# Splitting weights and context by way of a PSUM bank, in a decoder layer with a fusion layer behind it

## The chip, the cores and the metric

The kernel runs on one core of a Trainium2 chip. Its engines are TensorE (PE in the profile, with its weight loads as PEld), VectorE (DVE), ScalarE (ACT), GpSimd (POOL) and SyncE (SP), which here only issues transfers. The metric is device time in microseconds (us) of one execution. Before the change the median of three runs was 2229.88 us (2228.8 to 2230.53).

## The reference

The input `x` is 4 x 1024 x 512 in fp32, the context 4 x 64 x 512. A decoder layer comes first: self-attention with 16 heads of 32, causal, on a normalised `x`; attention to the context; a feed-forward part of width 2048. A fusion layer follows.

```python
xn1 = _ln(x, g1, be1)
sa = _mha(xn1, xn1, Wq_s, bq_s, Wk_s, bk_s, Wv_s, bv_s, causal=True)
x = x + (sa @ W1 + b1)
xn2 = _ln(x, g2, be2)
ca = _mha(xn2, encoder_out, Wq_c, bq_c, Wk_c, bk_c, Wv_c, bv_c, causal=False)
x = x + (ca @ W2 + b2)
xn3 = _ln(x, g3, be3)
ff = jax.nn.relu(xn3 @ Wf1 + bf1) @ Wf2 + bf2
return x + ff
```

The fusion layer projects the result with `Wt`, gates it with `Wg` (whose second half meets a pooled and projected context) and normalises the sum. Scores are divided by `DH ** -0.5`, so they are multiplied by about 5.7 before the softmax.

## The kernel before

Most products are made in three matmuls. Each operand is split into a high part, rounded to the type `fp32r`, and a low part, the rest; high x high, high x low and low x high are summed in one PSUM bank. A split is two instructions: ACT casts the source to the high part, and DVE subtracts the high part from the source (`split`, lines 70 to 74). Where the source is the result of a matmul it lies in PSUM. Where it is a weight or the context it lies in SBUF, and both operands of the subtraction are read from there.

The kernel has three phases: self-attention (0 to about 930 us), attention to the context, and the feed-forward and fusion part (from about 1,330 us). The change touches the first alone.

Self-attention has 32 units: four sequences, four groups of four heads, two sets of four row tiles. For each unit `maxima` makes scores (line 673) and their extremes on DVE (lines 678 and 681), `attend` makes the transposed scores (729), exponentials on ACT (734), a causal cut and a sum over key blocks on POOL (742 and 783) and the product with the values (759). The maxima of one unit, the attention of the one before and pieces of the projections for later units (`pk`, `pq`, `pv`, line 101) are traced interleaved by `run`, by their share of matmul columns. A planner then orders the instructions of each engine by a simulated timeline and each step's place in the trace; on the chip every engine works through its own queue in that order.

PSUM has eight banks. In this phase four belong to the tag `s` (pool `ps_s`, line 450), three to the transposed scores and one to the product with the values. Tiles of one tag take the banks in the order in which they were traced, and a tile waits until the last reader of the tile four places before it is done. The helper `psum` (467) hands out banks for projections and set-up; from line 857 on they are all of the tag `s`, shared with the maxima.

Two groups of splits of SBUF data lie beside the attention:

- `split_steps` (248 to 259): W1, Wq_c (with a sign of -1) and W2, four chunks of 128 x 512 each. A step loads a chunk through SP's queue into a tile `low`, makes `high` on ACT (255) and `low` in place on DVE (256), and stores both to DRAM through SP (258). The twelve steps are appended to the projection pieces from `pieces[8]` on, one per piece (894 and 895), together with steps that clear other DRAM tiles (897).
- the late set-up, in the last four units: `Stream` (line 280 issues its transfers) brings chunks of Wt, Wg, the context, Wk_c and Wv_c through ACT's queue into a ring of five tiles. `halve` (313) and `load_context` (389) split 16 weight chunks and four context chunks of 128 x 256 with `split`; then the products of the set-up are made. A ring tile is free for the next transfer when its last reader is done, which for these chunks is the subtraction on DVE.

The pieces of one unit's fill are traced behind each other, so that a step's place in the trace also sets which tiles of the tag `s` stand before and behind it.

Of the kernel before, what the change touches and what calls it, by code (L numbers as in the profile page):

```python
# [11 lines left out]
AF = mybir.ActivationFunctionType  # L12
ALU = mybir.AluOpType
# [5 lines left out]
B, T, C, H = 4, 1024, 512, 16  # L19
DH = C // H  # L20
S = 64
# [24 lines left out]
def raw(ap):  # L46

    return ap.bitcast(F32)
# [3 lines left out]
def decoder_then_fusion(ctx: ExitStack, tc: tile.TileContext, x, ctxT, cols, rows,  # L52
                        Wq_s, Wk_s, Wv_s, W1, Wq_c, Wk_c, Wv_c, W2, Wf1, Wf2,
                        Wt, WvT, WgT, out):
    nc = tc.nc
# [5 lines left out]
    def chunks(w):  # L61
        return w.rearrange("(c p) n -> p c n", p=P)
# [8 lines left out]
    def split(hi, lo, src, uid, lo_eng=None):  # L71

        latest["hi"] = nc.scalar.copy(hi, src).ins  # L73
        (lo_eng or nc.vector).tensor_tensor(lo, src, hi, ALU.subtract)  # L74

    def split_biased(hi, lo, src, bias):

        nc.scalar.activation(hi, src, AF.Identity, bias=bias)
        nc.vector.scalar_tensor_tensor(lo, src, bias, hi, ALU.add, ALU.subtract)
# [10 lines left out]
    def product_steps(psum_of, a, b, a_at, b_at, width, end, bias=None):  # L90


        held = {}

        def step(c):
            if c == 0:
                held["ps"] = psum_of()
                if bias:
                    nc.tensor.matmul(held["ps"], *bias(), start=True, stop=False)
            for k, (i, j) in enumerate(((0, 0), (0, 1), (1, 0))):  # L100
                nc.tensor.matmul(held["ps"], a_at(a()[i], c), b_at(b()[j], c),  # L101
                                 start=not bias and c == 0 and k == 0, stop=c == NC - 1 and k == 2)
            if c == NC - 1:
                end(held["ps"])

        per = Z["per"]

        def steps(c):
            for i in range(c, c + per):
                step(i)  # L110

        return [(3 * width * per, lambda c=c: steps(c)) for c in range(0, NC, per)]
# [21 lines left out]
    def behind(*engines):  # L134

        stack = ExitStack()
        for eng in engines:
            last = next(i for i in reversed(nc.cur_bb.bb.instructions) if i.engine == eng.engine)
            stack.enter_context(tc.issue_after(last))
        return stack  # L140
# [16 lines left out]
    def col(name, c):  # L157
        at = COL_AT[name] + c
        return colv[:, at : at + 1]
# [48 lines left out]
    def spread_keys(k, part):  # L208

        src = part.rearrange("p c (b s) -> p c b s", s=S)  # L210
        for r in range(HG):
            at = slice(r * DH, (r + 1) * DH)
            nc.sync.dma_start(kbd_dram[k, :, at, :, r * S : (r + 1) * S].rearrange("b p c s -> p c b s"), src[at])

    def spread_values(i, t):

        src = t.rearrange("p (n r d) -> p n r d", r=2, d=DH)
        for m in range(2):
            for k in range(2):
                nc.sync.dma_start(vbd_dram[k * S : (k + 1) * S, i * 2 + m, :, k * DH : (k + 1) * DH],  # L220
                                  src[m * S : (m + 1) * S, :, k, :])
# [23 lines left out]
    SPLIT = {"w1": (W1, 1.0), "wqc": (Wq_c, -1.0), "w2": (W2, 1.0)}  # L245
    split_dram = {k: dram.tile([P, 2, NC, C], F32, tag=f"{k}_d", name=f"{k}_d") for k in SPLIT}

    def split_steps(pool, slots):

        def step(name, c):  # L250
            w, sign = SPLIT[name]
            low, high = [pool.tile([P, C], FR, tag="chunk", name=f"{name}_{k}_{c}", bufs=slots) for k in "lh"]
            with behind(nc.sync):
                nc.sync.dma_start(raw(low), chunks(w)[:, c, :])
            nc.scalar.activation(high, raw(low), AF.Copy, scale=sign)
            nc.vector.scalar_tensor_tensor(low, raw(low), sign, high, ALU.mult, ALU.subtract)
            for k, t in enumerate((high, low)):
                nc.sync.dma_start(split_dram[name][:, k, c], raw(t))
        return [(0, lambda name=name, c=c: step(name, c)) for name in SPLIT for c in range(NC)]
# [38 lines left out]
    def setup(psum, rows_pool, stream):  # L298
# [9 lines left out]
        def halve(pool, name, tag, c):  # L308

            if c == 0:  # L310
                held[name] = [pool.tile([P, NC, C], FR, tag=f"{tag}{k}", name=f"{name}{k}") for k in range(2)]
            hi, lo = held[name]
            stream.take(lambda src: split(hi[:, c], lo[:, c], src, f"{name}_{c}"))

        def halve_small(name, src):

# [6 lines left out]
        def put(ps, m, bias, dst, uid):  # L323

            out_row = rows_pool.tile([P, C], F32, tag="side", name=f"side_{uid}", bufs=2)
            if bias is None:
                nc.vector.tensor_copy(out_row[:m], ps[:m])
            else:
                nc.vector.tensor_tensor(out_row[:m], ps[:m], held[bias][:m], ALU.add)
            held[f"row_{uid}"] = out_row  # L330
            if callable(dst):
                dst(out_row)
            else:
                nc.sync.dma_start(dst, out_row[:m])
# [48 lines left out]
        def context(pool):  # L383
            def load_context(c):
                if c == 0:
                    held["kcT"] = [pool.tile([P, NC, B * S], FR, tag=f"kcT{k}", name=f"kcT{k}") for k in range(2)]
                    held["ct"] = [pool.tile([P, NC, B * S], FR, tag=f"ct{k}", name=f"ct{k}") for k in range(2)]
                hi, lo = held["ct"]
                stream.take(lambda src: split(hi[:, c], lo[:, c], src, f"ct_{c}"))

            def keys(ps, g):
                split_biased(held["kcT"][0][:, g], held["kcT"][1][:, g], ps, col("bk_c", g))
                if g == NC - 1:
                    for k, t in enumerate(held["kcT"]):
                        spread_keys(k, raw(t))

            steps = [(0, lambda c=c: load_context(c)) for c in range(NC)]
            steps += [(0, lambda c=c: halve(pool, "wkc", "w", c)) for c in range(NC)]
            for g in range(NC):
                steps += product_steps(  # L400
                    lambda g=g: psum(f"pkc_{g}")[:, : B * S], lambda: held["wkc"], lambda: held["ct"],
                    lambda w, c, g=g: w[:, c, g * P : (g + 1) * P], lambda t, c: t[:, c, :], B * S,
                    lambda ps, g=g: keys(ps, g))
            steps += [(0, lambda c=c: halve(pool, "wvc", "w", c)) for c in range(NC)]
            for i in range(B * S // P):
                steps += product_steps(
                    lambda i=i: psum(f"pvc_{i}"), lambda: held["ct"], lambda: held["wvc"],
                    lambda t, c, i=i: t[:, c, i * P : (i + 1) * P], lambda w, c: w[:, c, :], C,
                    lambda ps, i=i: put(ps, P, "bv_c", lambda t: spread_values(i, t), f"vc{i}"))
            return steps  # L410
# [27 lines left out]
    def self_attention(ph):  # L438
# [16 lines left out]
        ring = ph.enter_context(tc.tile_pool(name="ring_a", reuse_waits="tile", bufs=1))  # L455
        stream = Stream(ring, Z["ring"])
# [10 lines left out]
        def psum(name):  # L467

            kind = early_banks[len(psum_count) % len(early_banks)]
            psum_count.append(name)  # L470
            return ps_of[kind][0].tile([P, TG], F32, tag=kind, name=name)
# [419 lines left out]
                stream.fill()  # L891


        for i, step in enumerate(split_steps(ring, Z["ring"])):
            pieces[2 * NC + i].append(step)
        pieces[Z["pf"]].append((0, prefetch))
        for i, step in enumerate(clear_steps(mask[:, : HG * S])):
# [651 lines left out]
    for phase in (self_attention, cross_attention, feed_forward):  # L1549
        with ExitStack() as ph:  # L1550
            phase(ph)
# [41 lines left out]
```

## Time and profile before

| | before |
|---|---|
| median of three runs | 2229.88 us |
| the profiled execution | 2229.15 us |
| its span, first to last instruction | 2227.4 us |
| mean granted clock of PE | 0.981 |
| PE, DVE, ACT, POOL busy | 2121.6, 1255.2, 983.7, 1070.6 us |
| line 255, high parts of w1, wqc, w2, on ACT | 12 instructions, 7.5 us |
| line 256, their low parts, on DVE | 12 instructions, 14.8 us |
| line 73, high parts of wt, wgt, wkc, wvc, ct | 20 instructions, 11.4 us |
| line 74, their low parts, on DVE | 20 instructions, 26.7 us |

The rows of the last four lines are sums over the groups of these tiles. The page of the profile lists engines, 40 slices of the span, transfers, the chain of waits and the costliest groups. A row of a group or of a source line names the line, the engine, the operation, output `<-` inputs, the count and the durations; a row of the timeline starts with start and duration in us and ends in brackets with the idle time before it and what ended it. `st`, `s`, `pT`, `top` and `least` are tiles of the attention. A granted clock of 1.00 is full speed of PE.

### The profile page before, as it was taken

How to read it: one execution, taken by the hardware profiler on the slowest of the kernel's cores; microseconds unless marked ns; L12 is line 12 of the kernel's file. 1: busy time of each engine (PE TensorE's matmuls, PEld its weight loads, DVE VectorE, ACT ScalarE, POOL GpSimd, SP SyncE). 2: the span in 40 equal slices, each digit the busy share in tenths (PEclk: the TensorE clock that was granted, in tenths of full speed). 3: DMA queues.
4: the chain of work that ended last, by engine and by line, in shares of the span. 5: the costliest groups of instructions: out<-in, count | busy, mean ns of one | idle time of the engine just before them, and what ended most of it. 6: DMA issues, size and time to landing. Idle time of an engine off the chain costs nothing.

```text
span 2227.4 us, 34074 instructions
## 1 busy us (share of the span) xinstructions
PE 2121.6 (95%) x11736; PEld 1606.5 (72%) x11736; DVE 1255.2 (56%) x2800; ACT 983.7 (44%) x2175; POOL 1070.6 (48%) x1139
## 2 busy tenths in 40 slices
PE   6899999999999999989999998999999999999997
PEld 5667665666666755558888886888887887888785
DVE  6566756765665578666677756341337225431727
ACT  3355545554655455435555565432233324232432
POOL 3178777787878778765555523010115103410414
PEclk9999999999999999999999999999999999999998
DMA  8856766676656467662323214644345525442631
GB/s 251 241 157 172 238 194 206 192 221 191 192 151 189 136 168 221 201 205 67 101 80 104 80 50 154 197 166 141 124 139 207 170 98 202 145 175 85 207 134 48
DMA packets 219427, 356.24 MB, mean 160 GB/s; under 512 B 33516, under 2 KB 101852, under 8 KB 217206
## 3 DMA queue, kind: packets, MB, share of 16 engines
q1 hardware_dynamic: 201548, 333.83, 48.0%
q10 hardware_dynamic: 17706, 20.24, 2.9%
q8 instruction: 93, 1.52, 0.3%
q14 instruction: 80, 0.66, 0.1%
HBM read 242.27 MB, written 111.18 MB: 159 GB/s over the span
## 4 chain that ended last, share of the span: by engine, by line
PE 67%; DMA 10%; DVE 10%; issue 6%; POOL 4%; ACT 3%; SPq 1%; DVEq 0%; ACTq 0%; POOLq 0%
PE ph_f L101 13%; PE acc_f L1331 13%; PE s L673 4%; PE st L729 4%; PE av L759 4%; PE po_c L101 3%; PE pq_x L101 3%; PE pk L101 3%; PE pg_o L101 3%; PE pq L101 3%; PE po_x L101 3%; POOL pT L783 3%; PE pv L101 2%; PE sc_c L86 2%; PE den L796 1%
## 5 line engine op out<-in xcount | busy, mean ns | idle before, releaser
L783 POOL TENSOR_TENSOR pT<-pT,pT 128x256 f32<-128x256 f32 (+3 forms) x369 | 547.4, 1504 | 98.4 <-PE av L759 85.0
L1331 PE MATMUL acc_f<-wf,hs_f 128*128 128x512 f32 x1536 | 384.9, 394 | 7.6 <-DVE hs_f L74 5.9
L734 ACT ACTIVATE pT<-st 128x512 f32<-128x512 f32 (+2 forms) x640 | 317.2, 561 | 158.0 <-PE st L729 101.3
L101 PE MATMUL ph_f<-xn_f,wf 128*128 128x512 f32 x1536 | 381.7, 393 | 3.3 <-DVE xn_f L74 2.6
L1331 PEld LDWEIGHTS acc_f<-wf,hs_f 128*128 128x128 f32 x1536 | 285.0, 188 | 71.0 <-DVE hs_f L74 8.1
L101 PEld LDWEIGHTS ph_f<-xn_f,wf 128*128 128x128 f32 x1536 | 287.8, 189 | 65.0 <-DVE xn_f L74 3.0
L678 DVE CUSTOM_DVE_ANT_0 s<-s,mask 128x512 f32<-128x512 f32 (+3 forms) x512 | 245.8, 502 | 118.8 <-PE s L673 118.0
L673 PE MATMUL s<-ks,qs 96*128 96x512 f32 (+3 forms) x768 | 250.8, 375 | 28.4 <-DVE top L681 8.3
L1310 ACT ACTIVATE ph_f<-ph_f,colv 128x512 f32<-128x512 f32 x128 | 84.4, 659 | 391.3 <-PE ph_f L101 387.2
L74 DVE TENSOR_TENSOR hs_f<-ph_f,hs_f 128x512 fp32r<-128x512 f32 x128 | 87.9, 686 | 285.6 <-ACT hs_f L73 285.6
L729 PE MATMUL st<-qs,ks 98*128 98x256 f32 (+2 forms) x888 | 231.1, 342 | 12.2 <-DMA qs<-mT 6.6
L681 DVE TENSOR_REDUCE top<-s 128x1 f32<-128x512 f32 x256 | 175.6, 686 | 108.5 <-PE s L673 108.1
L673 PEld LDWEIGHTS s<-ks,qs 96*128 96x128 f32 x768 | 140.5, 194 | 107.3 <-DVE top L681 23.1
L729 PEld LDWEIGHTS st<-qs,ks 98*128 98x128 f32 x888 | 150.0, 193 | 65.3 <-ACT pT L734 24.7
L1306 POOL TENSOR_TENSOR y_f<-y_f,row_bf 128x512 f32<-128x512 f32 x32 | 42.0, 1317 | 313.8 <-DMA y_f<-x 253.9
L742 POOL TENSOR_SCALAR_AFFINE_SELECT pT<-pT 128x256 f32<-128x256 f32 x256 | 106.0, 431 | 126.1 <-ACT pT L734 92.6
L759 PE MATMUL av<-pT,v 128*32 128x512 f32 (+3 forms) x1776 | 157.2, 455 | 5.1 <-POOL pT L742 4.6
L1446 POOL TENSOR_TENSOR g_o<-g_o,z_o 128x512 f32<-128x512 f32 x28 | 41.8, 1506 | 175.7 <-DVE g_o L1445 172.9
L101 PE MATMUL pv<-wv,xn_s 128*128 128x256 f32 x768 | 107.5, 290 | 6.7 <-ACT vout L578 5.4
L101 PEld LDWEIGHTS pv<-wv,xn_s 128*128 128x128 f32 x768 | 100.4, 194 | 18.3 <-ACT vout L578 6.0
L1082 POOL TENSOR_TENSOR p_c<-p_c,inv_c 128x512 f32<-128x512 f32 x64 | 68.8, 1076 | 87.1 <-DVE inv_c L1081 65.2
L101 PE MATMUL pk<-xn_s,wk 128*128 128x512 f32 x384 | 104.0, 412 | 1.6 <-ACT xn_s L73 0.8
(220 smaller groups left out, 3397.0 us busy)
## 6 DMA issues: line engine op xcount, KB each, us to landing
wf<-wf2d SPq DMA_DIRECT2D x84, 512.0 KB
ks<-kd SPq DMA_DIRECT2D x96, 256.0 KB
qs<-qd SPq DMA_DIRECT2D x96, 256.0 KB
kd<-k SPq DMA_DIRECT2D x64, 256.0 KB
qd<-q SPq DMA_DIRECT2D x120, 128.0 KB
wf<-wf1d SPq DMA_DIRECT2D x28, 512.0 KB
x<-in_x SPq DMA_DIRECT2D x32, 256.0 KB
wk<-wk SPq DMA_DIRECT2D x16, 512.0 KB
```

The lines of the kernel that those rows point to most:

```text
L74: (lo_eng or nc.vector).tensor_tensor(lo, src, hi, ALU.subtract)
L101: nc.tensor.matmul(held["ps"], a_at(a()[i], c), b_at(b()[j], c), start=not bias and c == 0 and k == 0, stop=c == NC - 1 and k == 2)
L673: nc.tensor.matmul(sc[:, :w], q_at[u][:KS, r, j * P : (j + 1) * P], k_at[u, m][:KS, r, :w], start=True, stop=True)
L678: nc.vector.tensor_tensor_reduce(sc[:, :w], sc[:, :w], mask[:, TG - w :], 1.0, TOP, ALU.add, ALU.min, dst)
L681: nc.vector.tensor_reduce(dst, sc, AX.X, ALU.min)
L729: nc.tensor.matmul(st[:, i], k_at[u, kb // NJ][:KM, r + i, (kb % NJ) * P : (kb % NJ + 1) * P], q_at[u][:KM, r + i, c0:], start=True, stop= ...
L734: nc.scalar.activation(held[kb][(r + i) // 2][:, at : at + k, c0:], st[:, i : i + k], AF.Exp, scale=-QSCALE)
L742: nc.gpsimd.affine_select(out=t, in_=t, compare_op=ALU.is_ge, fill=0.0, base=0, pattern=[[0, 2], [1, P]], channel_multiplier=-1)
L759: return nc.tensor.matmul(held["av"][r * DH : (r + 1) * DH, c0:], v_at[b, g][:, kb, r * DH : (r + 1) * DH], held[kb][r // 2][:, r % 2, c0: ...
L783: eng.tensor_tensor(t[:, :, c0:], t[:, :, c0:], p[:, :, c0:], ALU.add)
L1310: nc.scalar.activation(ps, ps, AF.Relu, bias=col("bf1", f))
L1331: mm = nc.tensor.matmul(acc[j], held[f][i0][:, j * P : (j + 1) * P], w[2, f][:, i1], start=f == 0 and m == 0, stop=last and m == 2)
```

## The change

A new helper `split_over` copies the source to a PSUM tile with a scale on ACT, and then calls `split` with that tile as the source. ACT thus makes the copy and the high part, DVE subtracts the high part from the tile in PSUM. It takes the place of the two instructions in `split_steps` and of `split` in `halve` and `load_context`. Each call takes a tile of `psum`, hence of the tag `s`. The sign, where there is one, goes into the copy.

```diff
+    def split_over(ps, hi, lo, src, uid, sign=1.0):
+
+
+        nc.scalar.activation(ps, src, AF.Copy, scale=sign)
+        split(hi, lo, ps, uid)
...
-    def split_steps(pool, slots):
+    def split_steps(pool, slots, psum):
...
-            nc.scalar.activation(high, raw(low), AF.Copy, scale=sign)
-            nc.vector.scalar_tensor_tensor(low, raw(low), sign, high, ALU.mult, ALU.subtract)
+            split_over(psum(f"{name}_{c}"), high, low, raw(low), f"{name}_{c}", sign)
...
-            stream.take(lambda src: split(hi[:, c], lo[:, c], src, f"{name}_{c}"))
+            stream.take(lambda src: split_over(psum(f"{name}_{c}"), hi[:, c], lo[:, c], src, f"{name}_{c}"))
...
-                stream.take(lambda src: split(hi[:, c], lo[:, c], src, f"ct_{c}"))
+                stream.take(lambda src: split_over(psum(f"ct_{c}")[:, : B * S], hi[:, c], lo[:, c], src, f"ct_{c}"))
...
-        for i, step in enumerate(split_steps(ring, Z["ring"])):
+        for i, step in enumerate(split_steps(ring, Z["ring"], psum)):
```

## The prediction

> **What bounds the kernel now.** I read the busy times first, then the two lines that the change rewrites, then the idle gaps of TensorE (PE) around them in the timelines, and last the granted clock there. The page and the timeline of VectorE (DVE), for one stretch in the attention:
>
> ```profile
> PE 2121.6 (95%) x11736; PEld 1606.5 (72%) x11736; DVE 1255.2 (56%) x2800; ACT 983.7 (44%) x2175; POOL 1070.6 (48%) x1139
> ...
> 355.12 4.99 DVE L256 SCALAR_TENSOR_TENSOR wqc_l<-wqc_l,wqc_h 128x512 fp32r<-128x512 f32 x1 [2.26 <-ACT wqc_h L255]
> ```
>
> PE is busy in 95% of the span, so only its idle time and its slow clock can be won. That one subtraction took 4.99 us, and its twin at 338.7 us took 0.69. The timelines of POOL and PE for the same stretch say why, and what it did:
>
> ```profile
> 353.26 5.95 POOL L783 TENSOR_TENSOR pT<-pT,pT 128x1024 f32<-128x1024 f32 x3
> ...
> 360.77 1.22 PE L673 MATMUL s<-ks,qs 96*128 96x512 f32 x2 [3.07 <-DVE top L681]
> ```
>
> POOL ran three additions back to back until 359.2, and the subtraction ended 0.9 us later. The score matmul of PE waited 3.07 us for the maximum queued behind it. The whole family, from the views of the two lines (min/median/max ns):
>
> ```profile
> L256 DVE SCALAR_TENSOR_TENSOR w_l<-w_l,w_h x8: 674/692/1223, 224.0 to 530.5; 128x512 fp32r<-128x512 f32 x8
> L256 DVE SCALAR_TENSOR_TENSOR wqc_l<-wqc_l,wqc_h x4: 689/1550/4994, 338.7 to 425.1; 128x512 fp32r<-128x512 f32 x4
> ...
> L74 DVE TENSOR_TENSOR xn_s<-tpn_s,xn_s x32: 656/692/694, 13.7 to 656.9; 128x512 fp32r<-128x512 f32 x32
> ...
> L74 DVE TENSOR_TENSOR wt<-chunk,wt x4: 681/946/2407, 819.5 to 835.7; 128x512 fp32r<-128x512 f32 x4
> L74 DVE TENSOR_TENSOR wgt<-chunk,wgt x4: 685/1599/2964, 820.1 to 839.5; 128x512 fp32r<-128x512 f32 x4
> ...
> L74 DVE TENSOR_TENSOR ct<-chunk,ct x4: 630/1150/1497, 866.3 to 871.3; 128x256 fp32r<-128x256 f32 x4
> L74 DVE TENSOR_TENSOR wkc<-chunk,wkc x4: 674/769/1754, 871.9 to 880.2; 128x512 fp32r<-128x512 f32 x4
> L74 DVE TENSOR_TENSOR wvc<-chunk,wvc x4: 886/1633/2650, 894.5 to 899.6; 128x512 fp32r<-128x512 f32 x4
> ```
>
> The `xn_s` row reads one operand from PSUM and never exceeds 694 ns, though POOL works through the same stages. The others read both operands from SBUF and are held. Busy time and clock by stretch:
>
> ```profile
> core 0: us, PE busy (x) PEld busy (x) DVE busy (x) ACT busy (x) POOL busy (x), PEclk, DMA share, GB/s
> ...
> 180.00:540.00 360.00, 337.43 (x2208) 232.70 (x2208) 229.91 (x651) 185.76 (x373) 274.48 (x287) 0.97 0.71 205
> 540.00:815.00 275.00, 270.20 (x1807) 187.11 (x1806) 174.05 (x531) 148.80 (x299) 220.86 (x224) 1.00 0.59 166
> 815.00:905.00 90.00, 80.65 (x469) 52.30 (x468) 72.98 (x153) 48.11 (x97) 74.26 (x64) 0.92 0.74 214
> ```
>
> The 12 splits of w1, wqc and w2 lie in the first stretch, the 20 of the late set-up in the third, none in the second. PE idles 6% and 10% of the time where splits are, 2% where none are. In the third stretch DVE is 81% busy and ScalarE (ACT) 53%.
>
> **What is removed.** The 32 subtractions cost 41.5 us of DVE in the table of groups (w_l 6.0, wqc_l 8.8, wt 5.0, wgt 6.8, ct 4.3, wkc 3.9, wvc 6.7). From PSUM they should cost 28 x 0.69 + 4 x 0.43 = 21.0 us (0.69 is the `xn_s` median; 0.43 the mean of the 128x256 maxima that read PSUM, 434 ns). DVE gives back 20.5 us. Of that only what PE waits for counts. The timelines of PE and DVE show idle time of PE right behind a held subtraction; from each gap I take no more than the excess of that subtraction over 0.69 us: 3.07 (at 357.7), 1.37 of 1.62 and 0.2 of 0.76 (823.6 to 826.4), 1.22 and 0.45 of 0.68 (837.6 to 840.7), 0.77 and 1.26 of 1.85 (870.5 to 874.1), 0.83 (898.3). Sum 9.2 us.
>
> The clock comes on top. The granted clock was 0.50 from 358.3 to 368.5, 826.0 to 832.8 and 873.8 to 880.6 us, each time just behind such gaps, with 7.73 + 6.37 + 6.49 = 20.6 us of PE busy in them. At full clock that work takes half, so 10.3 us are at stake. I take 5.1, the middle, because other gaps (0.97 us for a transfer of mT at 355) lie beside the held ones.
>
> Two gains I count at nothing. POOL's additions are stretched too (128x512: 1,283 ns before 815 us, 1,382 after; 128x1024: 2,400 and 2,553): some 7 us of POOL over its 64 rows there, hidden because PE waits for POOL under 1 us in that stretch. And a ring slot of a context or weight chunk comes free at the new ACT copy, not at the end of the DVE subtraction, so ACT, whose queue issues the next chunk's transfer, no longer stops for DVE: waits of 2.9, 1.7, 0.9, 0.8 and 0.6 us in the list of waits, 6.9 in all. That one is set against the copies below.
>
> **What is added.** 32 ACT copies from SBUF to PSUM. No row has that pair of memories. The 128x512 cast from PSUM takes 0.59 us, the scaled copy SBUF to SBUF (L255) 0.63, the scaled and biased PSUM to PSUM (L521) 0.76; by work L255 is nearest, so 28 x 0.63 + 4 x 0.40 (the 128x256 cast) = 19.2 us, with ends of 18.1 and 23.3. The cast behind the copy reads PSUM (0.59 for 0.62): nothing.
> - The early 12 add 7.6 us to ACT. In three of them PE waits for what stands behind the split on ACT or DVE: the gaps at 225.9 (1.22), 305.0 (2.40, ACT stood 1.74 for the weight's transfer) and 529.4 (2.24). Each grows by a copy: 1.9 us. The others lie beside other work of PE; without that cover it is 7.6. SP's queue holds two stores per split (24), and the first leaves a copy later; behind them stand the loads of the stacks. They lie two units ahead, and the stores now leave a held subtraction sooner (SP stood 4.1 us for one): zero, at worst inside the 7.6.
> - The late 20 add 11.6 us to ACT, less the 6.9 above: 4.7. Five splits come together at 818.7, ahead of the copy of the denominators, for which PE already waits 0.36 us. I put 3.0 of it on the path; ends 0 and 11.6.
> - The four score banks. Each split now holds one of them, taken in program order, from its copy to its subtraction. A bank freed late stops the fourth score or projection tile behind it. Where ACT stood for the weight's transfer (9 of 12 early splits, 15.3 us in all) PE can run one score tile less ahead. Price: one 128x512 score matmul, 0.43 us, nine times: 3.9 us. Ends: 0, and 32 x 0.43 = 13.8.
>
> Sum: -9.2 - 5.1 + 1.9 + 3.0 + 3.9 = -5.5 us. The profiled execution took 2229.15 us (span 2227.4, 1.75 around it), 0.7 below the median, so 2223.7 there and 2224.4 against the median; I say 2224.
>
> [...]
>
> **The rivals.**
> - Hidden anyway (within 0.2%): PE has the same 2,122 us of work and other waits take the place of the removed ones; next late would be ACT's exponentials, for which PE already waits 5.0 us from 180 to 960. For it: gaps behind transfers of mT (5.3 us) stay. Against it: the stretch without splits idles 2%. The time: 2226 to 2234, nearest 2229.
> - The score banks (slower): a split whose chunk has not landed holds a bank of four, and the scores and projections behind it stop. For it: projections, maxima and splits share these banks, and three late chunks were cast 9 us after the first five. Against it: DVE stopped at the same splits before. The gains are 9.2 + 5.1 = 14.3, the copies 4.9; it decides from (14.3 - 4.9 + 4.5) / 32 = 0.43 us lost per split on. With 0.65 us each, 20.8 in all, the time is 2229.9 + 11.4 = 2241.
> - Both sides of the gain without the cost (a faster end of my own case): idle and clock in full, 10.8 + 10.3 = 21.1, gives 2209.
> - The subtraction is held as before, since it still reads `hi` in SBUF and writes there: 2229.9 + 4.9 + 3.9 = 2239. Against it stands every PSUM row of L74, none over 694 ns.
>
> **How the numbers follow.** A change under 0.2% (4.5 us) can't be told from none. My case (the held subtractions go, the copies cost less) has 0.53: 0.45 of it faster than 2225.4, 0.08 within. Hidden anyway 0.17. The banks 0.25, the hold that stays 0.02, and 0.03 for ACT becoming what PE waits for (both copy sums in full, 19.2, against 14.3: 2235): these are slower. So faster 0.45, same 0.25, slower 0.30. My case alone spans 2209 to 2229; with the banks the range goes to 2243 (the gains 14.3 halved, 1.9 + 3.0 + 13.8 paid, is 2241.5, and a half-clock slot more).
>
> **What would show it.** Right: no subtraction of a split over 0.70 us; DVE down by 20, ACT up by 19 to 23; no PE gap of a microsecond behind L74 or the maxima between 355 and 362 or 820 and 875; fewer half-clock slots there; POOL's 128x512 row back to 1.29. Wrong: PE waits for a score bank whose last reader is a split, longer waits of PE for ACT, or new half-clock slots elsewhere, for the order of the work is planned anew from 200 us on.

## The result, and the profile after

The changed kernel takes 2268.14 us (median of 4; 2265.5 to 2273.71) against 2229.34 before: a ratio of 1.0178, interval 1.0158 to 1.0198. It is 39 us slower, where I forecast 6 us faster and a range that ended at 2243. The profiled execution took 2268.1 us, its span is 2266.4.

The busy times of the page, and then the rows of the two source lines of the new split (min/median/max ns):

```profile
PE 2149.3 (95%) x11736; PEld 1619.5 (71%) x11736; DVE 1227.7 (54%) x2800; ACT 997.6 (44%) x2207; POOL 1063.6 (47%) x1139
...
L74 DVE TENSOR_TENSOR w_l<-w,w_h x8: 674/686/695, 224.0 to 557.1; 128x512 fp32r<-128x512 f32 x8
L74 DVE TENSOR_TENSOR wqc_l<-wqc,wqc_h x4: 656/686/692, 344.8 to 435.6; 128x512 fp32r<-128x512 f32 x4
L74 DVE TENSOR_TENSOR wt<-wt,wt x4: 680/680/682, 856.1 to 870.4; 128x512 fp32r<-128x512 f32 x4
...
L74 DVE TENSOR_TENSOR wvc<-wvc,wvc x4: 681/681/691, 936.8 to 941.4; 128x512 fp32r<-128x512 f32 x4
...
L79 ACT ACTIVATE w<-w_l x8: 598/602/690, 221.5 to 554.6; 128x512 f32<-128x512 f32 x8
```

The instructions did what was forecast of them. No subtraction of a split is over 0.70 us, DVE is 27.5 us less busy, and the 32 copies cost 19.3 us. ACT's busy time rose by 13.9 us, less than the 19 to 23 forecast: its rows overlap in time, and their plain sum rose by 23.5. POOL's 128x512 additions took 1.28 us between 815 and 905 us, as forecast. PE, whose work is the same (x11736), is 28 us longer busy, at a mean granted clock of 0.971 (before 0.981). The stretches say where (engines' busy us, then the granted clock):

```profile
180.00:540.00 360.00, 332.23 (x2065) 225.47 (x2064) 207.56 (x618) 180.85 (x363) 253.72 (x265) 0.94 0.66 192
540.00:815.00 275.00, 267.60 (x1771) 185.31 (x1768) 163.29 (x494) 142.81 (x289) 215.95 (x218) 0.99 0.60 165
815.00:905.00 90.00, 79.93 (x444) 47.13 (x444) 51.20 (x149) 48.60 (x95) 70.49 (x69) 0.87 0.70 196
```

Between 180 and 540 us PE got 2,065 matmuls done, before 2,208. One matmul per unit transposes its maxima; its start is a milestone that both traces have. Against before it stands at -2.0 us at 215 us, +8.7 at 323, +15.9 at 440, +27.6 at 573, +28.8 at 821, +43.8 at 887 and +41.5 at 918. So some 29 us were lost where the twelve early splits are, nothing where there are none, and some 13 where the twenty late ones are. Milestones, here and below, come from one profiled execution of each kernel; these lay between 4.5 us below and 8.2 us above the median of their kernel, so single values are good to some microseconds only.

One early split in the timelines of SP, ACT, DVE and PE:

```profile
338.41 0.42 SPq L260 DMA_DIRECT2D wqc_l<-in_Wq_c  x1
```

```profile
343.56 0.60 ACT L79 ACTIVATE wqc<-wqc_l 128x512 f32<-128x512 f32 x1 [0.21 <-DMA wqc_l<-in_Wq_c]
```

```profile
334.69 0.69 DVE L686 TENSOR_REDUCE top<-s 128x1 f32<-128x512 f32 x1 [1.23 <-PE s L678]
344.81 0.69 DVE L74 TENSOR_TENSOR wqc_l<-wqc,wqc_h 128x512 fp32r<-128x512 f32 x1 [9.43 <-ACT wqc_h L73]
```

```profile
334.26 0.40 PE L678 MATMUL s<-ks,qs 96*128 96x512 f32 x1
...
335.81 1.72 PE L107 MATMUL pv<-wv,xn_s 128*128 128x256 f32 x13
337.37 0.87 PE L734 MATMUL st<-qs,ks 98*128 98x512 f32 x3
338.54 3.02 PE L734 MATMUL st<-qs,ks 98*128 98x512 f32 x9 [0.30 <-ACT pT L739]
341.63 1.06 PE L801 MATMUL den<-pT,ones 128*32 128x512 f32 x8
342.49 1.29 PE L764 MATMUL av<-pT,v 128*32 128x512 f32 x16
343.71 0.74 PE L734 MATMUL st<-qs,ks 98*128 98x256 f32 x4
344.29 0.34 PE L678 MATMUL s<-ks,qs 96*128 96x384 f32 x1
...
366.77 1.62 PE L734 MATMUL st<-qs,ks 98*128 98x512 f32 x3 [3.83 <-DMA qs<-mT]
```

The chunk's transfer is issued at 338.4, its copy runs at 343.6. Between the one that starts at 334.3 and the one at 344.3 PE has not one score matmul (`s`), and DVE stands 9.4 us. PE is not idle: it does the attention of the current unit. That comes back at the unit's end, where only the scores of the next one are left, and then their maxima and the transfer of mT have to be waited for: 3.83 us, and the granted clock was 0.50 from 363.3 to 373.5. Between 200 and 570 us there are 14 pauses of over 5 us from the start of one score matmul to the start of the next, 113 us together; before there were 5, with 30. Nine of the 14, with 83 us, end within 1.0 us of the start of an early split's copy; before, none ended so close to a cast of a split. From 180 to 640 us the gaps of PE grew from 25.3 to 32.8 us and the time at half clock from 20.5 to 51.2. In the changed kernel seven projection matmuls of 128x512 (`pk`) in a row took 3.18 us at a granted clock of 0.50 (from 401.4 us), eleven 2.72 at 1.00 (from 312.1): 0.45 and 0.25 us each. If the gaps were filled with matmuls, and half of the slow time won as in the prediction, the two would be an estimated 7.5 + 15.4 = 23 of the 29, at the measured ratio some 22.

The profile puts only 0.7 us of ACT's waits to these transfers (5.0 us more lie right before two of the copies and are put to a transfer of mT), and PE waits for the early splits' banks by nothing of note. The pause of the scores is in the order of PE's instructions, not in a wait of PE for a bank.

### The profile page after: what moved, and what is told of

It reads as the page before. It is cut to its first block, busy times and chain, and to the rows that moved or that the text cites. A ratio compares the mean times of both kernels' runs of the same rounds, so it can differ in the third digit from the quotient of the medians.

```text
span 2266.4 us, 34051 instructions
## 1 busy us (share of the span) xinstructions
PE 2149.3 (95%) x11736; PEld 1619.5 (71%) x11736; DVE 1227.7 (54%) x2800; ACT 997.6 (44%) x2207; POOL 1063.6 (47%) x1139
## 4 chain that ended last, share of the span: by engine, by line
PE 71%; DMA 8%; DVE 8%; issue 5%; POOL 4%; ACT 2%; SPq 1%; DVEq 0%; ACTq 0%; POOLq 0%
PE ph_f L107 12%; PE acc_f L1336 12%; PE st L734 5%; PE s L678 5%; PE av L764 5%; PE pk L107 4%; PE po_c L107 4%; PE pq L107 3%; PE pq_x L107 3%; PE pg_o L107 3%; PE po_x L107 3%; PE pv L107 3%; POOL pT L788 2%; PE sc_c L92 2%; DMA qs<-mT 2%
## 5 line engine op out<-in xcount | busy, mean ns | idle before, releaser
L107 PE MATMUL pk<-xn_s,wk 128*128 128x512 f32 x384 | 118.1, 454 | 1.8 <-ACT xn_s L73 0.8
L107 PEld LDWEIGHTS pv<-wv,xn_s 128*128 128x128 f32 x768 | 100.6, 194 | 15.3 <-DVE top L683 3.1
```

## The experiments

The theory from here on, the **order theory**: a split asks for its bank in trace order, while its chunk is still to be loaded. The planner places the tiles of the tag `s` one after the other, so until the copy can be placed, which waits for the transfer, no later score or projection is placed either. The planner's own timeline is not on record, so the theory is tested by what it foretells. The rivals: the extra **copies** on ACT; the **bank count**, one bank of four less for the scores while a split runs.

### The early and the late splits alone

Two kernels with the new split in one place and the old one in the other.

```diff
# e1: halve, load_context
-            stream.take(lambda src: split_over(psum(f"{name}_{c}"), hi[:, c], lo[:, c], src, f"{name}_{c}"))
+            stream.take(lambda src: split(hi[:, c], lo[:, c], src, f"{name}_{c}"))
# e2: split_steps
-            split_over(psum(f"{name}_{c}"), high, low, raw(low), f"{name}_{c}", sign)
+            nc.scalar.activation(high, raw(low), AF.Copy, scale=sign)
+            nc.vector.scalar_tensor_tensor(low, raw(low), sign, high, ALU.mult, ALU.subtract)
```

> Only the twelve splits of w1, wqc and w2 go through the bank; the twenty late ones are as before. Milestones of the two traces (the matmul that transposes the maxima of each unit) put +29 us between 215 and 575 us and +10 to +13 behind 821 us. If the two stretches are independent: +27 to +31 us against before, no new loss behind 821 us. If the loss is one of the whole plan (a different order everywhere), some other number, and no sum with the late-only kernel.

> Only the twenty late splits go through the bank. Independent stretches: no change of the milestones up to 800 us, +8 to +13 us at the end. If the late loss came from the state that the early one leaves behind: within 3 us of before or faster, since the held subtractions are gone.

Early alone: 1.0121 (1.0081 to 1.016), 2259.73 against 2230.3 us; the milestones end at +25.7. Late alone: 1.0039 (1.0024 to 1.0053), 2240.16 us; the milestones are within 2 us up to 821 and end at +13.9. The two parts add up to the whole, 29 + 10 = 39, as independent parts would.

### The chunk loaded one piece ahead

```diff
-        def step(name, c):
+        def load(name, c):
             w, sign = SPLIT[name]
-            low, high = [pool.tile(...) for k in "lh"]
+            held[name, c] = [pool.tile(...) for k in "lh"]
             with behind(nc.sync):
-                nc.sync.dma_start(raw(low), chunks(w)[:, c, :])
+                nc.sync.dma_start(raw(held[name, c][0]), chunks(w)[:, c, :])
+
+        def part(name, c):
+            w, sign = SPLIT[name]
+            low, high = held[name, c]
             split_over(psum(f"{name}_{c}"), high, low, raw(low), f"{name}_{c}", sign)
...
+            pieces[2 * NC + i + 1].append(step)   # the parts, one piece later
+            pieces[2 * NC + i].append(step)       # the loads
```

A load keeps its place in the trace, and its split moves to the next piece. In e3 the late splits go through the bank too, in e5 they are as before.

> As the changed kernel, but the chunk of an early split is loaded one projection piece (some 25 us) before the piece that copies it to the bank. Order theory (a bank tile is asked for in trace order, and while its copy waits for a transfer no later score or projection tile may be placed): the early +29 us vanishes, so +7 to +13 us against before, and the milestones are within 4 us of before up to 800 us. Theory of the copies (32 more instructions on ACT) and theory of the bank count (one bank of four less while a split runs): nothing is won, still +35 to +42.

> The early splits with their chunk loaded a piece ahead and through the bank; the late ones as before. In the kernel with both, the milestones stood 17 us ahead of before at 800 us and lost 14 of it behind 821 us. If the stretches are independent: -12 to -18 us against before (2212 to 2218). If the late loss there had another cause than the late splits through the bank: no better than -9.

e3: 0.9967 (0.9951 to 0.9984), 2222.84 against 2230.3. e5: 0.9907 (0.9876 to 0.9939), 2215.68 against 2230.66. For e3 that is better than the order theory had expected, and neither the copies nor the bank count can be the cause of the early loss by themselves: they are all still there. e5 against the kernel with the early splits alone (e1) differs in nothing but where the split stands behind its load, and that turns 29 us lost into 15 won. The milestones of e5 stand at -15.1 at 800 us. The first stretch of e5:

```profile
180.00:540.00 360.00, 349.94 (x2349) 243.59 (x2349) 233.25 (x685) 201.58 (x404) 289.94 (x301) 0.99 0.73 212
```

2,349 matmuls, where the kernel before had 2,208 and the changed one 2,065. Three score pauses over 5 us are left (17.7 us), and from 180 to 640 us gaps of PE of 13.7 us and 6.8 us at half clock. e5 beats both kernels.

### A copy without a bank, a bank without a transfer

e4 makes the extra copy in place in SBUF. e7 splits as before and takes a bank besides, filled from a mask that is always there.

```diff
# e4
-            split_over(psum(f"{name}_{c}"), high, low, raw(low), f"{name}_{c}", sign)
+            split_over(raw(low), high, low, raw(low), f"{name}_{c}", sign)
# e7, behind the two old instructions of the split
+            spare = psum(f"spare_{name}_{c}")
+            nc.scalar.activation(spare, mask, AF.Copy)
+            unused = small.tile([P, 1], F32, tag="unused", name=f"unused_{name}_{c}", bufs=2)
+            nc.vector.tensor_reduce(unused, spare, AX.X, ALU.min)
```

> The early splits make the same extra copy on ACT, in place in SBUF and not in a bank; the late ones are as before. Theory of the copies: most of the early loss stays, +15 to +30 us. Order theory and bank count: -3 to +6 us (a copy of 0.6 us in twelve places, subtractions still held by POOL).

> As before in all splits, and each early step takes a score bank besides, fills it on ACT from a mask that lies in SBUF since the start, and reads it on DVE into a column that nobody uses: the bank, the copy and one more DVE instruction, but no transfer in front of the bank. Order theory: 0 to +8 us (the twelve extra instructions on ACT and DVE and a bank held for 2 us each). Bank-count theory: +15 us and more, near the +29 of the early splits through the bank.

e4: 1.0045 (1.002 to 1.0071). That is more than the order theory had given, and the milestones show +11 at 800 us, in an execution that lay 5.6 us above its median. In this kernel ACT stands 19.8 us for the chunks' transfers (15.3 before), with the longer chain behind them. So a copy right behind a transfer seems to cost something, at most some 11 of the 29 us; in e5, where the same twelve copies follow a chunk that has long landed, they cost nothing that shows.

e7: 1.0032 (1.0013 to 1.0051), within what the order theory gave. Its milestones stand at +3.1 at 800 us; the rest came in the late part, which this edit does not touch. Twelve banks, each held 1.3 to 6.0 us from its filling to its last read (2.0 to 5.3 in the changed kernel) but with no transfer in front, are no +29.

### What e5 wins: the hold or the transfer

A subtraction is called held here when it lasts well over its 0.69 us while POOL works. Two kernels have the early load but the old two instructions from SBUF. In e6 nothing else is changed. The planner moved its splits forward again: they stand at 223 to 338 us, 4 to 10 us behind the issue of their transfers (e5: 249 to 537 us, over 20 behind). e6 therefore does not part the two causes. e9 pins the high part behind the last ACT instruction traced, and its splits then stand at 252 to 573 us, 13 to 38 behind.

```diff
# e9
+            with behind(nc.scalar):
                 nc.scalar.activation(high, raw(low), AF.Copy, scale=sign)
```

> The chunk is loaded a piece ahead, but the early splits are made from SBUF as before, in two instructions; the late ones as before. This parts the gain of the earlier load from that of the bank. If the bank's own worth is what I predicted for the early part (3 us of idle time and some 4 of the clock behind one held subtraction): the load alone gives -4 to -10, and e5 is 3 to 10 us faster than this. If the bank is worth nothing: equal to e5 within 2 us. If the load alone is worth nothing: within 3 us of before.

> As the kernel with the early load and splits from SBUF, but the high part of an early split is ordered behind the last ACT instruction traced, so that the split stands as late as in e5, a piece behind its transfer. No wait for transfers and no bank; the subtractions can still be held by POOL. If what e5 wins is the hold: subtractions of 1.5 to 5 us stay, and the time lies 8 to 15 us above e5, -7 to +1 against before. If what e5 wins is the wait for transfers: within 4 us of e5, -11 to -15.

e6: 1.0003 (0.9982 to 1.0024). e9: 1.0037 (1.0018 to 1.0056), 2240.79 against 2232.72, so 8 us slower than before and about 23 behind e5. This is past the worst that I had given it. The rows of its subtractions, and the longest one with POOL and PE beside it:

```profile
L269 DVE SCALAR_TENSOR_TENSOR w_l<-w_l,w_h x8: 681/942/6993, 252.0 to 572.5; 128x512 fp32r<-128x512 f32 x8
...
L269 DVE SCALAR_TENSOR_TENSOR wqc_l<-wqc_l,wqc_h x4: 676/3567/11884, 353.5 to 450.1; 128x512 fp32r<-128x512 f32 x4
```

```profile
353.52 11.88 DVE L269 SCALAR_TENSOR_TENSOR wqc_l<-wqc_l,wqc_h 128x512 fp32r<-128x512 f32 x1
```

```profile
354.36 0.40 POOL L756 TENSOR_SCALAR_AFFINE_SELECT pT<-pT 128x256 f32<-128x256 f32 x1
354.73 1.27 POOL L797 TENSOR_TENSOR pT<-pT,pT 128x512 f32<-128x512 f32 x1
355.96 0.40 POOL L756 TENSOR_SCALAR_AFFINE_SELECT pT<-pT 128x256 f32<-128x256 f32 x1
356.34 2.33 POOL L797 TENSOR_TENSOR pT<-pT,pT 128x1024 f32<-128x1024 f32 x1
358.63 0.40 POOL L756 TENSOR_SCALAR_AFFINE_SELECT pT<-pT 128x256 f32<-128x256 f32 x1
359.00 5.85 POOL L797 TENSOR_TENSOR pT<-pT,pT 128x1024 f32<-128x1024 f32 x3
```

```profile
366.06 1.58 PE L687 MATMUL s<-ks,qs 96*128 96x512 f32 x3 [10.10 <-DVE top L695]
```

The subtraction ended 0.55 us after POOL's run of work, at 364.85, and PE stood 10.1 us. The twelve subtractions took 37.5 us in place of the 8.2 of e5. Between 180 and 640 us PE has gaps of 33.8 us in e9 (profiled 7.9 us above its median), and three of them, 4.0, 10.1 and 5.0 us, lie behind held subtractions; what is left, 14.7, is near the 13.7 of e5. So at these places the hold is what e5 is spared.

Against the kernel before, the two causes are not parted. Of the 25.3 us of gaps there only 3.6 lie behind a held subtraction, and e5 has 11.6 us of gaps less. PE's waits for ACT's exponentials fell from 5.1 us to none of note, and where ACT stood 15.3 us for the chunks before, it stands for none in e5. Both the hold and the transfers fit what e5 wins. What a hold cost differed with where the subtraction fell in POOL's work: at the places of the kernel before, three of the twelve were held (1.22, 2.41 and 4.99 us), at those of e9 seven by over 0.1 us, the longest 11.88.

### The late splits

In e8 the three splits whose transfers are issued inside the set-up are made from SBUF; the other 17 go through the bank. In e10 and e11 the steps ahead of the first product are traced further apart, through the bank and from SBUF.

```diff
# e8, in halve
+            if (name, c) in (("wgt", 2), ("wt", 3), ("wgt", 3)):
+                stream.take(lambda src: split(hi[:, c], lo[:, c], src, f"{name}_{c}"))
+                return
# e10 and e11
-'lat': [0.2, 1.0, 0]
+'lat': [1.5, 1.0, 0]
```

> Only late splits go through the bank, and of these not the three (the third chunk of wgt, the fourth of wt and wgt) whose transfers are issued inside the set-up itself. Order theory alone: the +9 of all late splits through the bank shrinks to between -3 and +3. If the late loss is from crowding (splits traced back to back take the four banks and ACT): it stays at +5 to +10.

> Late splits through the bank, and the twelve steps ahead of the first set-up product are traced seven times as far apart (a share of 1.5 in place of 0.2), so that more scores stand between two splits. To be read against e11, which spreads the same steps and splits from SBUF. If the late loss is crowding, with transfers that the copies wait for: no more than +3 against e11. If the late splits lose through the bank wherever they stand: +6 to +12 against e11.

> The kernel before with the same wider spread of the late steps. The control of e10: the spread itself may cost or win up to 8 us, since work of the set-up moves to later units.

e8: 1.0021 (0.9999 to 1.0043); e10: 1.0014 (0.9991 to 1.0036); e11: 1.0018 (0.9996 to 1.004). The interval of e8 reaches from nothing into that of e2 and settles nothing by itself. The milestones of units 28 and 31 (counted from 0) bound the stretch of the late splits: it takes 110 to 113 us in the three kernels with all late splits through the bank and the old spread, 108 in e8, 103 in both e10 and e11, and 98 to 107 in the seven others with late splits from SBUF (98 to 102 without e7). But holds differ between these kernels too. In e8 one of the three splits that were put back to SBUF is held (DVE, then PE):

```profile
831.41 8.93 DVE L74 TENSOR_TENSOR wgt<-chunk,wgt 128x512 fp32r<-128x512 f32 x1
```

```profile
840.93 0.79 PE L682 MATMUL s<-ks,qs 96*128 96x512 f32 x1 [7.85 <-DVE least L687]
```

So e8 gives up one loss for another and does not tell what the three transfers cost. In e7, whose late code is that of before, a subtraction of `wgt` took 8.57 us (2.96 the longest before), and another DVE instruction on SBUF data, `sa_x`, 7.08; PE stood 5.8 and 5.1 us behind them, where no gap in this stretch was over 1.9 us before. So its late part got longer by holds that fell elsewhere. In e11, 14.5 us of PE's 17.6 us of gaps in this stretch lie behind held subtractions (8.1 of 9.3 before); in e10, whose splits are not held, the gaps are 13.9 us.

What is left is this: with the splits traced further apart, the stretch through the bank takes 103 us in place of 110 to 113, still some 5 more than before, and the control e11, with its holds, takes 103 too. That fits crowding, splits traced back to back that take the four banks together, but it is not shown. In the changed kernel and in e2 PE's longest waits from 815 to 940 us are for POOL's causal cut (4.7 and 7.4 us) and for mT (2.1 and 3.1 us), none for a bank. The cause of the late loss stays open.

## Why the prediction was wrong

- **The subtractions and DVE: right.** I gave 0.69 us each and 20.5 us of DVE; none is over 0.695, and DVE has 27.5 us less, of which these subtractions give 21.1.
- **The copies: right in size.** 19.2 us forecast, 19.3 measured. That they cost little on the path was seen for landed chunks only (e5); right behind a transfer (e4) they may have cost up to 11 us.
- **The score banks: the failed step.** I priced them at 0.43 us for nine splits, 3.9 us, with an upper end of 13.8, by the reasoning that PE could run one score tile less ahead. The early splits cost 29 us, some 2.4 each. It is not a matter of how many banks are left (e3, e5 and e7 speak against that): where the bank tile is asked for ahead of its data, the scores pause for 5 to 13 us at a time until the copy runs, nine times. That the planner's placing does this is the reading that fits all these runs; its timeline was not seen. The rival named the place, a split whose chunk has not landed, but with 0.65 us each it ended at 2241. What I held against it, that DVE stopped at the same splits before, was true and beside the point: before, no pause of the scores ended at a split. The front part of this document says that tiles take banks in trace order; I did not carry that to the time between asking for a bank and filling it.
- **The gain: right in kind, by chance near in size.** 14.3 us gross over both parts, of which only 3.1 us of gap and 1.9 of clock lay in the early part; e5 wins 15 with the early part alone. The gaps from 180 to 640 us fell by 11.6 and the half clock by 13.7 us, by an estimate at half of it up to 6.9 us of work. My way of counting it, gap by gap at the places of before, does not hold: e9 shows that at other places the holds cost 29 us of DVE over twelve unheld subtractions, where before it was 6.5. The 6.1 us of gap forecast for the late part were won in no run: with no late split held, the stretch was longer than before (103 to 113 us, before 98).
- **The late part: wrong, and open.** I had it faster by the late gaps and their clock, with 3.0 us of copies against them. It is 10 to 13 us slower, and no run settles by what.
- **The ring slots that come free earlier, a gain on ACT: seen in its waits, not in the time.** Waits of the kind that I counted, 6.9 us, are 1.0 us after, but the late stretch got longer.

## What to carry to other kernels

Where tiles of a tag are placed in trace order, a tile that is filled from memory should be asked for when its data has landed, not when its transfer is issued: the early part of this change is 29 us slower or 15 us faster on this account. A pause of one kind of work need not show as a wait; count how long that kind is absent from an engine, and follow milestones that both traces have. And a subtraction with both operands in SBUF should be priced by the run of POOL's work that it falls into, not by its shortest row: in e9 twelve of the same size took 0.68 to 11.88 us.

## What the runs showed of the hardware

DVE's wait was not over with the POOL instruction that was running: in e9 the 0.69 us subtraction took 11.88 us, across the end of one POOL instruction and eight more in a row, the longest of these 2.33 us, and ended 0.55 us after the last. In all profiled runs 68 subtractions of splits of 128x512, between 180 and 1,000 us and with both operands in SBUF, took over 1.2 us, and every one ended 0.54 to 0.55 us after the end of a POOL instruction. Nine of them are in the kernel before, 1.22 to 4.99 us. Behind the three additions that the prediction saw, POOL ran one more cut, until 359.6, and the subtraction of 4.99 us ended at 360.1:

```profile
359.15 0.43 POOL L742 TENSOR_SCALAR_AFFINE_SELECT pT<-pT 128x256 f32<-128x256 f32 x1
```

A subtraction of a split that reads one operand from PSUM took 0.694 us at most in the kernel before and 0.695 in the changed kernel. A copy on ACT from SBUF to PSUM took 0.60 to 0.76 us for 128x512 in the changed kernel, where the nearest row before, SBUF to SBUF, was 0.63.
